# Expert gates brought to the features' partitions by DRAM transfers, and max-with-0 and gate product as one DVE operation

## Chip, cores and metric

The kernel runs on one core of a Trainium2 chip. The metric is the device time of one execution in microseconds (us). The core's engines work in parallel, each through its own queue in order: PE (matrix products), DVE (vector operations), ACT (functions and copies), POOL (a second, general vector engine) and SP, which here only issues DMA transfers. SBUF and PSUM are the on-chip memories; matrix products end in PSUM[...].

## What is computed

Eight layers run over an input of 8 blocks of 512 tokens with 128 features, in fp32. The change concerns the sixth, an expert layer with 32 experts of 64 features each, of which every token uses four. Cut to what matters:

```python
def _L2_ffn_ref(x, expert_sel, keys, values):   # x: tokens x 128
    sel_logits = jnp.einsum('nd,ed->ne', xt, expert_sel)
    gates = jax.nn.sigmoid(sel_logits)
    sel_val, sel_idx = jax.lax.top_k(gates, 4)
    gate_full = jnp.zeros_like(gates).at[jnp.arange(N)[:, None], sel_idx].set(sel_val)
    scores = jax.nn.relu(jnp.einsum('nd,edf->nef', xt, keys))
    scores = scores * gate_full[:, :, None]
    out = jnp.einsum('nef,efv->nv', scores, values)
    return out.reshape(B, S, -1)
```

and `x = x + _L2_ffn_ref(_layernorm(x), ...)`. All 32 experts are computed for all tokens; the 28 gates that weren't chosen are zero. The seventh layer, a scan over time, follows.

## The kernel before

The function l2_ffn_l3_attn (L1138) holds the sixth and the seventh layer. Its first part, from L1336, is the stage of this study. It works block by block (b from 0 to 7). Features stand on the partitions and the 512 tokens of a block along the free dimension. Two experts of 64 features fill the 128 partitions, so a block has 16 pairs (j from 0 to 15).

For each pair: PE multiplies the pair's keys with the normalised block xT (L1432) into a PSUM tile mm; ACT takes the maximum with 0 into act (L1436); DVE multiplies act with the gates (L1444); and PE adds the pair's value product to acc (L1421, in add_up). The list late holds pairs whose value product isn't issued yet: it is issued once more than one pair waits, so that PE computes key products ahead.

The gates must stand on the feature rows: each of the two experts' gates, one number for each token, on 64 partitions. For this PE multiplies a 0/1 matrix sel with the transposed gates gT (L1443), for four pairs at once (every fourth j), in four PSUM tiles sp. The four products use 32 rows of the array each, so that gT holds the gates four times, on rows 0, 32, 64 and 96. POOL builds sel once, ahead of the stage (L1341, L1344).

The gates come from route(b) (L1371), a generator: normalise, transpose, logits on PE, sigmoid on ACT, then four times first_max (L1350) on DVE, which finds and removes the largest gate of each token; then the gates are copied four times (full4, L1393), transposed on PE and copied by ACT into gT (L1399). route(0) runs ahead of the loop; route(b + 1) runs beside block b. Such generators lie in the list side, and each pair ends with step(side) (L1448), which lets each of them run to its next yield. Others there: give_back (L1404: acc is transposed, added to X, and the statistics for the next norm are taken on DVE), folded, and prepare (L1273), which makes the scan's inputs for blocks 0 and 1 beside blocks 5 and 6: a chain on PE, ACT and then POOL, which ends with two writes to DRAM on SP's queue, dt_d (4 MB, L1327) and du_d (2 MB, L1331).

The code states an order of issue; the compiler orders the instructions of each engine by it and by when it expects their inputs, and each engine then runs its queue in order. PSUM in this stage: two tiles mm (shared by key products and everything in side), two acc, four sp.

After the stage the scan begins (L1455), which reads dt_d and du_d back in transfers dr, gx and xk (fetch, L1466).

Of the kernel before, what the change touches and what calls it, by code (L numbers as in the profile page):

```python
# [15 lines left out]
F32 = mybir.dt.float32  # L16
AF = mybir.ActivationFunctionType
ALU = mybir.AluOpType
# [21 lines left out]
def eight_layers(ctx: ExitStack, tc: tile.TileContext, w: dict, out: bass.AP):  # L40
# [184 lines left out]
    def flipped(src, ps, dst, scale=None):  # L225

        for c in range(C):
            nc.tensor.transpose(ps[:, c, :], src[:, c, :], ident)
        flat = ps.rearrange("p c t -> p (c t)")
        if scale is None:  # L230
            nc.scalar.copy(dst, flat)
        else:
            nc.scalar.activation(dst, flat, AF.Copy, scale=scale)
# [904 lines left out]
    def l2_ffn_l3_attn():  # L1138
# [18 lines left out]
        with ExitStack() as es:  # L1157
# [178 lines left out]
            with ExitStack() as es2:  # L1336
                ffn = es2.enter_context(tc.tile_pool(name="f2", bufs=2))
                ps2 = es2.enter_context(tc.tile_pool(name="f2p", bufs=2, space=PSUM))

                sel = ffn.tile([P, 4, 2, 64], F32, tag="sel", name="sel", bufs=1)  # L1340
                nc.gpsimd.memset(sel, 1.0)  # L1341
                for k in range(4):
                    at = sel[32 * k : 32 * k + 32]
                    nc.gpsimd.affine_select(  # L1344
                        out=at, in_=at, compare_op=ALU.is_equal, fill=0.0, base=-2 * k,
                        pattern=[[-8, 4], [-1, 2], [0, 64]], channel_multiplier=1,
                    )
                ready = {}

                def first_max(sc, last):  # L1350
# [20 lines left out]
                def route(b):  # L1371
                    r = rstd_of(mv2, b)
                    yield True
                    xn = ffn.tile([P, C, D], F32, tag="xn", name="xn")
                    normal(b, mv2, r, xn)
                    yield True
                    xT = ffn.tile([P, S], F32, tag="xT", name="xT")
                    flipped(xn, mm_four(), xT)
                    yield True
                    lp = mm_four()[:, :, 0:E]  # L1380
                    for c in range(C):
                        nc.tensor.matmul(lp[:, c, :], xT[:, cols(c)], f2_sel, start=True, stop=True)
# [11 lines left out]
                    nc.vector.tensor_tensor(  # L1394
                        full4, full.unsqueeze(2).to_broadcast([P, C, 4, E]),
                        oh.unsqueeze(2).to_broadcast([P, C, 4, E]), ALU.add,
                    )
                    yield True
                    gT = ffn.tile([P, S], F32, tag="gT", name="gT")  # L1399
                    flipped(full4.rearrange("p c k e -> p c (k e)"), mm_four(), gT)  # L1400
                    ready[b] = xT, gT
                    yield True

                def give_back(b, acc):  # L1404
                    oT = ffn.tile([P, S], F32, tag="oT", name="oT")
# [7 lines left out]
                    yield True  # L1413

                finish(route(0))
                side = [folded()]
                late = []

# [4 lines left out]
                        side.append(give_back(b, acc))  # L1423

                for b in range(NB):
                    xT, gT = ready.pop(b)
                    if b < NB - 1:
                        side.append(route(b + 1))
                    acc = ps2.tile([P, S], F32, tag="acc", name="acc")
                    for j in range(J):  # L1430
                        mm = mm_tile()
                        nc.tensor.matmul(  # L1432
                            mm, f2_k[:, 2 * j : 2 * j + 2, :], xT, start=True, stop=True
                        )
                        act = ffn.tile([P, S], F32, tag="act", name="act", bufs=4)
                        nc.scalar.activation(act, mm, AF.Relu)  # L1436
                        if len(late) > 1:
                            add_up()
                        if j % 4 == 0:
                            sp = [ps2.tile([P, S], F32, tag="sp", name="sp", bufs=4) for k in range(4)]  # L1440
                            for k in range(4):
                                at = slice(32 * k, 32 * k + 32)
                                nc.tensor.matmul(sp[k], sel[at, j // 4], gT[at], start=True, stop=True)  # L1443
                        nc.vector.tensor_tensor(act, act, sp[j % 4], ALU.mult)  # L1444
# [281 lines left out]
```

## Time and profile before

| What | Value |
|---|---|
| Median of 3 runs | 2018.02 us (2016.74 to 2020.12) |
| Profiled execution | 2007.65 us |
| Its span, first to last instruction | 2005.9 us |
| Mean granted clock of PE | 0.853 |
| Busy shares: PE, DVE, ACT, POOL | 83%, 64%, 41%, 33% |
| Stage of this study: first key product to last value product | 953.6 to 1262.9 us of the span |

A line of the timeline has the start in us, the duration in us, the engine, the line of code, the operation, what it writes and reads, shapes and how often, and in brackets how long the engine was idle before it and what ended that. Product groups with x2 are one fp32 product in two passes. A line of groups ends with busy time and mean duration in ns, and the idle time just before the group with what released it. PE's products overlap, so that its busy time can't be added up; starts can.

### The profile page before, as it was taken

To read this page: it belongs to the slowest core of one execution; us is meant where nothing else is said; L and a number is where in the kernel's file an instruction comes from. 1 tells how busy PE (TensorE), PEld (TensorE's weight loads), DVE (VectorE), ACT (ScalarE), POOL (GpSimd) and SP (SyncE) were. 2 spreads that over 40 slices of the span, in tenths; PEclk is the share of its full clock that TensorE was granted. 3 is DMA by queue.
4 is the path that set the end of the run, shared out by engine and by line. 5 is a ranking of instruction groups with operands and counts; after the bars stand their busy time and mean duration, and the time that the engine had idled before them with its cause. 6 is when DMAs were issued, how large, how long until landed. Compare 5 with 4: busy or idle time off the path is not lost.

```text
span 2005.9 us, 24650 instructions
## 1 busy us (share of the span) xinstructions
PE 1661.1 (83%) x9157; PEld 688.7 (34%) x9157; DVE 1283.0 (64%) x2369; ACT 826.5 (41%) x1197; POOL 655.8 (33%) x708
## 2 busy tenths in 40 slices
PE   6978988999989775785999999698768788698774
PEld 2322333434444363554434444112112112122353
DVE  5656666566655422454565554498878779798489
ACT  4645555544534221442323343345445346345221
POOL 5544433432211204303020054516245244211152
PEclk8989989888999997776999999758778778677788
DMA  8970000000000272000000024653864855842000
GB/s 277 383 222 1 1 1 11 17 10 9 21 16 17 88 223 61 18 1 0 1 0 1 0 79 173 193 156 107 227 192 92 246 169 131 236 111 74 1 16 27
DMA packets 118345, 181.02 MB, mean 90 GB/s; under 512 B 11464, under 2 KB 43088, under 8 KB 118224
## 3 DMA queue, kind: packets, MB, share of 16 engines
q1 hardware_dynamic: 116176, 175.24, 29.4%
q0 software_dynamic: 2048, 4.20, 0.7%
q8 instruction: 72, 1.18, 0.2%
q14 instruction: 49, 0.40, 0.1%
HBM read 74.55 MB, written 96.47 MB: 85 GB/s over the span
## 4 chain that ended last, share of the span: by engine, by line
PE 24%; DVE 14%; issue 5%; DMA 4%; POOL 4%; ACT 1%; SPq 1%; DVEq 0%; POOLq 0%; ACTq 0%
DVE h L1599 5%; PE bx L1588 5%; PE mm L1432 4%; PE acc L1421 4%; DMA dr<-dt_d 3%; PE Z L1501 3%; PE sp L1443 1%; POOL h L1637 1%; DMA gx<-du_d 1%; PE o L1641 1%; DVE act L1444 1%; DVE t L1652 1%; PE mm L1520 1%; SPq L1472 1%; DVE n L1654 1%
## 5 line engine op out<-in xcount | busy, mean ns | idle before, releaser
L1599 DVE TENSOR_TENSOR_SCAN h<-a,bx 128x1024 f32<-128x1024 f32 x192 | 427.9, 2270 | 98.4 <-ACT a L1594 53.0
L1594 ACT ACTIVATE a<-dr,nA 128x1022 f32<-128x1022 f32 x192 | 216.6, 1144 | 308.4 <-DVE h L1599 191.7
L1588 PE MATMUL bx<-gx,wb 32*64 32x512 f32 x1536 | 233.8, 814 | 94.0 <-DVE h L1599 55.1
L1444 DVE TENSOR_TENSOR act<-act,sp 128x512 f32<-128x512 f32 x128 | 87.6, 686 | 128.7 <-ACT act L1436 84.1
L1488 POOL TENSOR_TENSOR gx<-gx,xk 128x1024 f32<-128x1024 f32 x32 | 75.3, 2353 | 253.5 <-DMA gx<-du_d 222.4
L1501 PE MATMUL Z<-h,wc 64*32 64x512 f32 x1536 | 147.5, 830 | 10.5 <-DVE zx L1509 10.3
L1436 ACT ACTIVATE act<-mm 128x512 f32<-128x512 f32 x128 | 76.2, 597 | 164.7 <-PE mm L1432 155.7
L1421 PE MATMUL acc<-act,L_ffn_values 128*128 128x512 f32 x256 | 132.9, 602 | 8.2 <-DVE act L1444 8.1
L1432 PE MATMUL mm<-xT,L_ffn_keys 128*128 128x512 f32 x256 | 135.3, 610 | 0.0
L1588 PEld LDWEIGHTS bx<-gx,wb 32*64 32x64 f32 x1536 | 42.2, 159 | 260.3 <-DVE h L1599 182.5
L470 DVE TENSOR_REDUCE mx<-sm 128x8 f32<-128x1024 f32 x64 | 76.2, 1212 | 46.8 <-POOL sm L466 46.8
L498 POOL TENSOR_SCALAR_AFFINE_SELECT eT<-eT 128x1024 f32<-128x1024 f32 x64 | 68.6, 1095 | 105.6 <-ACT eT L496 105.5
L466 POOL TENSOR_SCALAR_AFFINE_SELECT sm<-sm 128x1024 f32<-128x1024 f32 x64 | 69.3, 1096 | 56.7 <-ACT sm L465 56.3
L496 ACT ACTIVATE eT<-sT 128x1024 f32<-128x1024 f32 x64 | 62.0, 1020 | 57.9 <-PE sT L489 57.8
L465 ACT COPY sm<-sc 128x1024 f32<-128x1024 f32 x64 | 63.0, 1013 | 51.3 <-PE sc L459 31.6
L1178 POOL TENSOR_TENSOR rstd<-rstd,minus_half 128x4 f32<-128x4 f32 x16 | 16.5, 1036 | 192.0 <-DVE rstd L1177 191.9
L459 PE MATMUL sc<-kb,qT 32*128 32x512 f32 x256 | 58.4, 736 | 22.4 <-ACT eT L496 10.2
L321 DVE SCALAR_TENSOR_TENSOR xn<-x,mv,rstd 128x128 f32<-128x128 f32 x128 | 45.9, 409 | 44.5 <-POOL rstd L317 44.4
L1421 PEld LDWEIGHTS acc<-act,L_ffn_values 128*128 128x128 f32 x256 | 47.1, 192 | 65.2 <-issue 46.5
L489 PE MATMUL sT<-qT,kb 32*128 32x512 f32 x256 | 57.1, 692 | 14.2 <-ACT sm L465 8.3
L1432 PEld LDWEIGHTS mm<-xT,L_ffn_keys 128*128 128x128 f32 x256 | 46.2, 192 | 65.2 <-issue 52.1
L199 DVE BATCH_NORM_STATS2 bn<-x 128x6 f32<-128x128 f32 x256 | 64.2, 271 | 6.5 <-DMA x<-in_L_attn_hidden_states 5.4
(411 smaller groups left out, 3203.9 us busy)
## 6 DMA issues: line engine op xcount, KB each, us to landing
f_in<-we SPq DMA_DIRECT2D x10, 3584.0 KB, 27.2
dt_d<-dt SPq DMA_DIRECT2D x8, 4096.0 KB, 13.0
dr<-dt_d SPq DMA_DIRECT2D x64, 512.0 KB, 7.9
du_d<-du SPq DMA_DIRECT2D x8, 2048.0 KB, 14.0
gx<-du_d SPq DMA_DIRECT2D x32, 512.0 KB, 6.5
wt<-in_L_ffn_experts SPq DMA_DIRECT2D x48, 192.0 KB, 2.8
xk<-xh SPq DMA_DIRECT2D x128, 64.0 KB, 6.1
xg<-f_in SPq DMA_DIRECT2D x48, 64.0 KB, 2.6
```

What stands on the lines that cost most here:

```text
L466: nc.gpsimd.affine_select(out=sm, in_=sm, compare_op=ALU.is_ge, fill=-1e30, base=0, pattern=[[0, 8], [-1, P]], channel_multiplier=1,)
L470: nc.vector.tensor_reduce(mx[:, c, 2 * i : 2 * i + 2, 0:4], sm.rearrange("p (q r) k -> p q r k", q=2), AX.X, ALU.max, negate=True,)
L498: nc.gpsimd.affine_select(out=e4, in_=e4, compare_op=ALU.is_ge, fill=0.0, base=0, pattern=[[0, 8], [1, P]], channel_multiplier=-1,)
L1421: nc.tensor.matmul(acc, f2_v[:, j, :], act, start=(j == 0), stop=(j == J - 1))
L1432: nc.tensor.matmul(mm, f2_k[:, 2 * j : 2 * j + 2, :], xT, start=True, stop=True)
L1436: nc.scalar.activation(act, mm, AF.Relu)
L1444: nc.vector.tensor_tensor(act, act, sp[j % 4], ALU.mult)
L1488: nc.gpsimd.tensor_tensor(gx, gx, xk.unsqueeze(1).to_broadcast([P, 2, S]), ALU.mult)
L1501: nc.tensor.matmul(zs[q][32 * j : 32 * j + 32, i, :], wc[half, g, :], hs[j // 2][half, j % 2, :], start=(g == 0), stop=(g == G - 1),)
L1588: nc.tensor.matmul(bx[64 * i : 64 * i + 64, k, :], wb[at, g, :], gx[at, i, :], start=True, stop=True,)
L1594: nc.scalar.activation(a[:, :, 1:], dr[:, 2 * j : 2 * j + 2, 1:], AF.Exp, scale=nA[:, q, g : g + 1],)
L1599: nc.vector.tensor_tensor_scan(h.rearrange("p r t -> p (r t)"), a.rearrange("p r t -> p (r t)"), bx.rearrange("p r t -> p (r t)"), 0.0, AL ...
```

## The change

The gates are transposed once, on 32 rows, copied to gT and written to DRAM (gd, 64 KB for each block). For each group of four pairs fetch_gates reads them back into a tile gate, twice 64 partitions, each row repeated 64 times: two transfers of 512 KB on SP's queue. It is issued two groups ahead, and there are three such tiles. At pair 8 of each block this asks for the next block's gates, so that route is stepped on until they are issued. sel, its products and full4 go. The maximum with 0 and the gates' product become one DVE operation that reads the key product from PSUM; ACT has no part in it. Key products get four PSUM tiles of their own (key) in place of sp. The value product lags by three pairs in place of two, and act has five buffers in place of four.

```diff
-                sel = ffn.tile([P, 4, 2, 64], F32, tag="sel", name="sel", bufs=1)
-                nc.gpsimd.memset(sel, 1.0)
-                for k in range(4):
-                    at = sel[32 * k : 32 * k + 32]
-                    nc.gpsimd.affine_select(
-                        out=at, in_=at, compare_op=ALU.is_equal, fill=0.0, base=-2 * k,
-                        pattern=[[-8, 4], [-1, 2], [0, 64]], channel_multiplier=1,
-                    )
...
                     full = first_max(gt, False)
-                    for k in range(1, 3):
+                    for k in range(1, 4):
                         yield True
-                        oh = first_max(gt, False)
+                        oh = first_max(gt, k == 3)
                         nc.vector.tensor_tensor(full, full, oh, ALU.add)
                     yield True
-                    oh = first_max(gt, True)
-                    full4 = ffn.tile([P, C, 4, E], F32, tag="full4", name="full4")
-                    nc.vector.tensor_tensor(
-                        full4, full.unsqueeze(2).to_broadcast([P, C, 4, E]),
-                        oh.unsqueeze(2).to_broadcast([P, C, 4, E]), ALU.add,
-                    )
-                    yield True
-                    gT = ffn.tile([P, S], F32, tag="gT", name="gT")
-                    flipped(full4.rearrange("p c k e -> p c (k e)"), mm_four(), gT)
-                    ready[b] = xT, gT
-                    yield True
+                    mm = mm_four()
+                    for c in range(C):
+                        nc.tensor.transpose(mm[0:E, c, :], full[:, c, :], ident)
+                    gT = ffn.tile([E, S], F32, tag="gT", name="gT", bufs=1)
+                    nc.scalar.copy(gT, mm[0:E].rearrange("p c t -> p (c t)"))
+                    gd = dram.tile([E, S], F32, tag="gates", name="gates", bufs=3)
+                    nc.sync.dma_start(gd, gT)
+                    ready[b] = xT, gd
+                    yield True
+
+                spread = {}
+
+                def fetch_gates(b, m):
+
+                    gd = ready[b][1]
+                    t = ffn.tile([P, 4, S], F32, tag="gate", name="gate", bufs=3)
+                    for k in range(2):
+                        nc.sync.dma_start(
+                            t[64 * k : 64 * k + 64],
+                            gd[8 * m + k : 8 * m + 8 : 2, :].unsqueeze(0).to_broadcast([64, 4, S]),
+                        )
+                    spread[b, m] = t
...
                 finish(route(0))
+                fetch_gates(0, 0)
+                fetch_gates(0, 1)
...
                     for j in range(J):
-                        mm = mm_tile()
+                        if j % 4 == 0:
+                            m = 4 * b + j // 4 + 2
+                            if m < 4 * NB:
+                                while m // 4 not in ready:
+                                    step(side)
+                                fetch_gates(m // 4, m % 4)
+                            gate = spread.pop((b, j // 4))
+                        key = ps2.tile([P, S], F32, tag="key", name="key", bufs=4)
                         nc.tensor.matmul(
-                            mm, f2_k[:, 2 * j : 2 * j + 2, :], xT, start=True, stop=True
-                        )
-                        act = ffn.tile([P, S], F32, tag="act", name="act", bufs=4)
-                        nc.scalar.activation(act, mm, AF.Relu)
-                        if len(late) > 1:
+                            key, f2_k[:, 2 * j : 2 * j + 2, :], xT, start=True, stop=True
+                        )
+                        act = ffn.tile([P, S], F32, tag="act", name="act", bufs=5)
+                        nc.vector.scalar_tensor_tensor(
+                            act, key, 0.0, gate[:, j % 4, :], ALU.max, ALU.mult
+                        )
+                        if len(late) > 2:
                             add_up()
-                        if j % 4 == 0:
-                            sp = [ps2.tile([P, S], F32, tag="sp", name="sp", bufs=4) for k in range(4)]
-                            for k in range(4):
-                                at = slice(32 * k, 32 * k + 32)
-                                nc.tensor.matmul(sp[k], sel[at, j // 4], gT[at], start=True, stop=True)
-                        nc.vector.tensor_tensor(act, act, sp[j % 4], ALU.mult)
                         late.append((b, j, act, acc))
```

More of the change, by code (lines that the diff above doesn't have):

```diff
@@ L1425, in l2_ffn_l3_attn @@
                 for b in range(NB):
[L1426 removed]
+                    xT = ready[b][0]
                     if b < NB - 1:
                         side.append(route(b + 1))
[L1429 removed]
+                    acc = ps2.tile([P, S], F32, tag="acc", name="acc", bufs=2)
                     for j in range(J):
[L1431 removed]
+                        if j % 4 == 0:
[6 more added lines that the diff above has]
+                        key = ps2.tile([P, S], F32, tag="key", name="key", bufs=4)
                         nc.tensor.matmul(
[L1433 removed]
+                            key, f2_k[:, 2 * j : 2 * j + 2, :], xT, start=True, stop=True
                         )
[L1435 to L1444 removed]
+                        act = ffn.tile([P, S], F32, tag="act", name="act", bufs=5)
[3 more added lines that the diff above has]
+                        if len(late) > 2:
+                            add_up()
                         late.append((b, j, act, acc))
```

## The prediction

> **What bounds the kernel now.** I read the page's engine shares first, then the groups by line, then the order of time on PE inside the stage that the change touches (the second expert layer, 953.6 to 1262.9 us of the span), then the waits, and last the transfers. The stage's own row and the groups:
>
> ```profile
> 950.00:1263.00 313.00, 299.50 (x949) 127.97 (x949) 171.62 (x454) 102.92 (x176) 65.80 (x77) 0.98 0.11 41
> L1432 PE MATMUL mm<-xT,L_ffn_keys 128*128 128x512 f32 x256 | 135.3, 610 | 0.0
> L1443 PE MATMUL sp<-gT,sel 32*128 32x512 f32 x256 | 42.6, 644 | 0.0
> L1444 DVE TENSOR_TENSOR act<-act,sp 128x512 f32<-128x512 f32 x128 | 87.6, 686 | 128.7 <-ACT act L1436 84.1 <-PE sp L1443 44.6
> ```
>
> The columns of the first are PE, weight loads, DVE, ACT, POOL, then clock, DMA share and GB/s. PE is busy for 299.5 of 313 us at a clock of 0.98, DVE for 172, ACT for 103, and the transfers use 11%. DVE waits for PE and ACT, so PE sets the pace. Busy time overlaps, so I take PE's pace from the starts:
>
> ```profile
> 1062.48 1.14 PE L1443 MATMUL sp<-gT,sel 32*128 32x512 f32 x8
> 1063.55 1.13 PE L1432 MATMUL mm<-xT,L_ffn_keys 128*128 128x512 f32 x2
> 1064.51 1.02 PE L1421 MATMUL acc<-act,L_ffn_values 128*128 128x512 f32 x2
> 1065.37 1.02 PE L1432 MATMUL mm<-xT,L_ffn_keys 128*128 128x512 f32 x2
> ...
> 1068.80 1.02 PE L1432 MATMUL mm<-xT,L_ffn_keys 128*128 128x512 f32 x2
> 1069.66 1.02 PE L1421 MATMUL acc<-act,L_ffn_values 128*128 128x512 f32 x2
> 1070.61 1.14 PE L1443 MATMUL sp<-gT,sel 32*128 32x512 f32 x8
> ```
>
> A pair of experts (one key product, one value product) takes 1.715 us: 1065.37 to 1068.80 is two of them. A group of four pairs with its gate products takes 1070.61 - 1062.48 = 8.13 us, so these cost 8.13 - 4 x 1.715 = 1.27 us of PE's time, with nothing beside them. Where PE does stand still, DVE is behind:
>
> ```profile
> 1049.89 1.13 PE L1421 MATMUL acc<-act,L_ffn_values 128*128 128x512 f32 x2 [2.48 <-DVE act L1444]
> 1055.05 0.63 PE L228 MATMUL mm<-ident,full 128*128 128x128 f32 x4 [0.54 <-DVE full L1394]
> ```
>
> That is the burst of top-four selections (first_max) in pairs 4 to 8 of each block. The stage's account: 309.3 = 128 x 1.715 (219.5) + 32 x 1.27 (40.6) + the side products (routing 1.75 x 7, giving back 0.44 x 8, prepare 5.7 x 2, the folded weights 0.6: 27.8), which leaves about 21 us of waits, of which 18 are such bursts and the rest the cold start and the tail.
>
> **What the Trainium skill says.** "VectorE: DVE Perf Modes", section on why PSUM operands drop a tier: a PSUM operand holds an fp32 operation at one element per cycle. The trace agrees for the operation removed (686 ns for 512 with one operand in PSUM). "SBUF — State Buffer", section on who interferes with whom: a DVE operation with at most one SBUF input doesn't contend with GpSimd. Both the old and the new multiplication have one; no run here isolates it. "DMA: Bandwidth & Descriptors", section on queues, rings and completion order: a sequencer's transfers go into one ring per engine and are consumed in ring order. The trace agrees: du_d, 2 MB, issued 1.35 us after the 4 MB dt_d, lands after 14.0 us and dt_d after 13.0. "TensorE: Matmul & The Clock Gate", section on what is actually happening: after an idle window of about 3.4 us the clock halves. The first key products agree: two passes from 953.56 to 955.41, 1.85 us in place of 0.86.
>
> **The change part by part.**
>
> *Gate products go.* 32 groups x 1.27 us. The first lies in the start-up, which I treat apart: 31 x 1.27 = -39.4 us, all on PE's path.
>
> *ACT's maximum goes, DVE's operation changes.* DVE does 128 operations as before. The new form (three operands, key in PSUM) isn't there at 512; L1652, all in SBUF, takes 684 ns, L1117 with PSUM takes 342 at 128 where the same operation in SBUF takes 290 to 338. I take 0.69 us; the bounds are 0.68 and 0.74. DVE's sum stays near 170 us, below PE's. ACT loses 128 x 0.6 us, which lay beside PE: nothing by itself, but the way from key to act is some 0.8 us shorter. Key products get four PSUM tiles of their own (the four of sp), so that side products no longer share two with them; the 7.1 us that weight loads of L1432 waited for ACT's act are small pieces beside running products, and I count nothing for them. full4 (0.69) becomes an addition of 0.28.
>
> *Start-up.* Now:
>
> ```profile
> 934.57 2.89 POOL L1344 TENSOR_SCALAR_AFFINE_SELECT sel<-sel 32x512 f32<-32x512 f32 x4
> 937.54 3.12 POOL L1178 TENSOR_TENSOR rstd<-rstd,minus_half 128x4 f32<-128x4 f32 x3
> 953.81 0.58 ACT L231 COPY gT<-mm 128x512 f32<-128x512 f32 x1 [10.52 <-PE mm L228]
> 956.95 0.69 DVE L1444 TENSOR_TENSOR act<-act,sp 128x512 f32<-128x512 f32 x1 [4.41 <-PE sp L1443]
> ```
>
> Building sel holds the power operation that starts routing: without it 2.5 us sooner, and 0.4 for full4, so gT is there at 954.4 - 2.9 = 951.5. Then gates go to DRAM (64 KB; f_in->xg takes 2.6, xT 2.0: I take 2.3) and come back (two issues of 0.58, landing after some 7.5, from dr's rows below): about 961.4, and the first value product at 962.3. By then four key products are done, 4 of the block's 32. The old kernel had 4 of 32 done at 961.84. So +0.5, and +1.5 for a clock that may fall while PE waits: **+2**.
>
> *The steady supply.* A group's gates are 1 MB in two transfers, of the same size and packets as dr's:
>
> ```profile
> dr<-dt_d SPq DMA_DIRECT2D x64, 512.0 KB, 7.9
> 1266.00:1276.00 10.00, 6.25 (x28) 2.03 (x26) 0.19 (x2) 3.05 (x5) 4.43 (x5) 1.00 0.91 211
> dt_d<-dt SPq DMA_DIRECT2D x8, 4096.0 KB, 13.0
> du_d<-du SPq DMA_DIRECT2D x8, 2048.0 KB, 14.0
> ```
>
> In the second line, where such reads fill the engines to 0.91, they give 211 GB/s: 1.05 MB in 5.0 us, below the 6.9 us of a group. With three buffers, the transfer starts when DVE has finished the group two before and has 13.7 us less DVE's lag of 2 to 6. It fits with a landing of 8. The source is four rows read 64 times each; the nearest such read, out_proj_b (64 KB from one row of 512 B), lands in 2.9 us, and out_proj_w of the same size without repetition in 3.2. I take no penalty. The new waits: on SP the fetch waits for the gates' write and for a buffer, with only later fetches and prepare's writes queued behind it; on DVE act waits for its gate, and behind it stand the selections, the additions to X and, for PE, the value product three pairs later.
>
> *Bursts.* In pairs 4 to 8 DVE has about 2.3 us of selection to each 0.69 of product, against PE's 1.715. The gate products gave PE two pieces of other work there (2.5 us) and go; sums that lag by three pairs in place of two (1.7) and the shorter way (0.8) return as much. But the transposition of the gates now stands before pair 8's key product, because the fetch of the next block's gates must follow it. If PE really waits there, up to 2.8 us of cover (key, value and gate products at 1051 to 1054) are lost per block: at most +20 over seven blocks. If the deeper queues absorb the bursts, -10. I take **+6**.
>
> *Gates behind prepare's writes.* SP also issues dt_d and du_d, which wait for POOL. In the trace dt_d went out 7.0 us after block 6 began (1192.00 against 1185.02); with blocks shorter, about 9. A fetch behind both on SP is issued near 14 and drains behind 15.4 us of writes: landing at 28 to 29 us. In block 6 group 2 is wanted at about 23 and PE can run 3.5 on: 2 us lost. In block 7, without side work, it is wanted at 15.3 and PE runs 4 on: 9 lost. If SP issues the fetch first, nothing. Between 0 and +11; I take **+5**. Were a fetch of group 1 behind them, each would cost 16.
>
> After the stage nothing changes; the scan's loads wait for its last products as now.
>
> *Sum:* -39.4 + 2 + 6 + 5 = **-26.4 us**. The profiled execution has a span of 2005.9 and took 2007.65, 10 below the median of 2018.02. I subtract from the median: **1992**.
>
> **Rivals.**
> 1. Everything hides: bursts cost what they cost now, fetches go ahead of prepare's writes: -39.4 + 2 = -37, with absorption down to -47: **1981**. For it: 11% DMA share. Against: DVE's bursts already stop PE.
> 2. PE waits for DVE at the transposition and for gates in blocks 6 and 7: -39.4 + 2 + 20 + 11 = -6: **2012**. For it: the 2.48 us wait above.
> 3. Slower: gate supply becomes the bound. Repeated reads of the same 8 KB by 16 engines could be slower than 211 GB/s. An old group takes 309.3 / 32 = 9.67 us; the change loses once 1.05 MB takes longer than that, below 108 GB/s. At 100 GB/s, 32 x 10.5 = 336: +27, **2045**. For it: no read of this shape at this size in the trace. Against: out_proj_b.
>
> **How the numbers follow.** Forecast 0.50 (its own range 1980 to 2004), rival 1 0.15, rival 2 0.17, rival 3 0.18. Range 1970 to 2022: rival 1's absorption to rival 2 with a fetch one group later; most of rival 3 is left out. A measurement can tell 0.2% (4 us). Rivals 1 and 2 and the forecast are faster except a tail of rival 2: faster 0.77, same 0.05, slower 0.18.
>
> **What would show it.** No sp row; group periods near 6.9 us; DVE's act at 0.69; first act near 961; gate landings near 8 us; waits of PE for DVE in pairs 4 to 8 and at the transposition; act waiting for a gate in block 7 after dt_d. Wrong would be: landings of 10 us and more in every group with DVE waiting for DMA, or PE waits of over 7 us per block.

## The result and the profile after

The changed kernel takes 1996.7 us (median of 4 runs, 1995.6 to 1998.0), the kernel before on the same chip 2018.9 us (4 runs, 2016.7 to 2020.1): a ratio of 0.9891, 95% interval 0.9874 to 0.9909, or 22 us less. The forecast was 1992 us, the range 1970 to 2022.

The new rows of the stage, first of the groups by line, from the reference point to the end of the stage (busy us, mean ns, then idle time just before and what ended it):

```profile
L1443 PE MATMUL key<-xT,L_ffn_keys 128*128 128x512 f32 x256 | 135.6, 614 | 0.0
L1425 PE MATMUL acc<-act,L_ffn_values 128*128 128x512 f32 x256 | 134.8, 611 | 19.6 <-DVE act L1447 19.6
L1447 DVE SCALAR_TENSOR_TENSOR act<-key,gate 128x512 f32<-128x512 f32 x128 | 85.5, 685 | 98.2 <-PE key L1443 51.0 <-DMA gate<-gates 41.3 <-PE mm L228 5.7
```

and of the transfers (KB each, median us from issue to landing):

```profile
gate<-gates SPq DMA_DIRECT2D x64, 512.0 KB, 10.3
gates<-gT SPq DMA_DIRECT2D x8, 64.0 KB, 1.6
```

No sp row is left. DVE's fused operation takes 685 ns, as its predecessor did (686). New are 41.3 us in which DVE waits for gates (36.7 of them in blocks 6 and 7, 4.6 once in block 1), and 19.6 us in which a value product of PE waits for DVE: the forecast has to be checked there. In the middle of the stage PE runs as forecast; the order of time on PE:

```profile
1021.30 1.02 PE L1425 MATMUL acc<-act,L_ffn_values 128*128 128x512 f32 x2
1022.16 1.02 PE L1443 MATMUL key<-xT,L_ffn_keys 128*128 128x512 f32 x2
1023.02 1.02 PE L1425 MATMUL acc<-act,L_ffn_values 128*128 128x512 f32 x2
```

A pair takes 1.72 us (1021.30 to 1023.02) with nothing between pairs, so a group takes 6.9 us in place of 8.13. Block 3 as a whole, from its first value product to that of block 4, in the view by stretches, first before, then after (length, busy PE, weight loads, DVE, ACT, POOL, clock, DMA share, GB/s):

```profile
1074.40:1111.50 37.10, 35.71 (x118) 15.31 (x117) 22.20 (x64) 11.59 (x20) 2.90 (x5) 1.00 0.00 0
```

```profile
1065.60:1095.60 30.00, 30.00 (x88) 14.14 (x87) 20.63 (x66) 2.12 (x5) 2.79 (x5) 1.00 0.65 139
```

PE was busy for 35.71 of 37.10 us, and is now busy all the time for 30.00 us. The transfers fill 0.65 of the engines and hide.

To see where the rest went I took the start of each block's first value product, counted from one point that both kernels share: the first of the last four operations of L1117, in which the attention layer before the stage adds to X (932.57 us before, 937.53 after; the 5 us between them lie in code that is the same in both). After the stage both take the same again, 743.1 and 743.7 us. The time from this point to the last line of the table is called the length of the stage below.

| us from the reference point | before | after | difference |
|---|---|---|---|
| first value product of block 0 | 25.1 | 33.2 | |
| of block 1 | 64.1 | 63.5 | -0.6 |
| of block 6 | 258.0 | 222.2 | five blocks: -35.2 |
| start of the last value product's second pass | 329.7 | 312.1 | two blocks: +18.2 |
| sum | | | -17.6 |

The stage gains 17.6 us in the traces, and the medians differ by 22. The traces don't explain the other 4 us. They are no more than code that is the same varies by: the part after the stage takes 739.6 to 747.0 us in the traces of all kernels here.

Blocks 1 to 5 gain 7 us each on average (6.3 to 8.4), blocks 6 and 7 lose 18 us together though their eight groups of products are gone too. These two blocks by stretches:

```profile
1159.70:1178.00 18.30, 15.30 (x50) 7.60 (x49) 15.31 (x45) 2.93 (x4) 11.64 (x14) 0.96 0.65 240
1178.00:1191.00 13.00, 9.00 (x17) 3.54 (x14) 0.67 (x2) 4.34 (x6) 5.39 (x6) 0.76 1.03 266
1191.00:1208.50 17.50, 17.42 (x36) 7.50 (x36) 4.58 (x8) 0.59 (x1) 12.65 (x12) 0.83 0.42 126
1208.50:1224.10 15.60, 0.03 (x2) 0.02 (x1) 2.84 (x12) 0.00 (x0) 1.02 (x1) 0.57 0.97 273
1224.10:1250.20 26.10, 26.10 (x56) 11.24 (x56) 9.70 (x15) 0.00 (x0) 0.00 (x0) 0.93 0.68 179
```

PE does nothing for 15.6 us (1208.5 to 1224.1) and stands for 4 in the second stretch; after each stop its clock is down (0.76, 0.83, 0.93 as means), so that products of 0.86 us a piece take longer. The cause stands in the order of SP, which issues both the gates and prepare's writes:

```profile
1165.31 0.56 SPq L1327 DMA_DIRECT2D dt_d<-dt  x1
1166.67 3.15 SPq L1331 DMA_DIRECT2D du_d<-du  x1
1169.91 10.73 SPq L1400 DMA_DIRECT2D gate<-gates  x4
1180.74 1.40 SPq L1389 DMA_DIRECT2D gates<-gT  x1
1203.17 0.55 SPq L1327 DMA_DIRECT2D dt_d<-dt  x1
1203.82 8.68 SPq L1400 DMA_DIRECT2D gate<-gates  x4
1212.62 1.32 SPq L1331 DMA_DIRECT2D du_d<-du  x1
1214.05 14.19 SPq L1400 DMA_DIRECT2D gate<-gates  x4
```

and in SP's waits in that window (total, times, longest):

```profile
SPq L1327 <- POOL dt L1325: 38.6, 2, 21.0
```

The write of block 7's gates to DRAM is issued at 1180.74. Not one of their eight fetches goes out in the 21.0 us after it: SP is in order, the next thing on it is dt_d of block 1, and POOL has dt ready only at 1203.1. In the first 12 us of these 21.0 the gates weren't all in DRAM yet: their write stood last in the queue, behind the writes of block 0 and the fetches of block 6, and the last packet of these transfers ends at 1194.5. After that nothing moves (the last two columns are DMA share and GB/s):

```profile
1194.00:1195.00 1.00, 1.00 (x3) 0.48 (x2) 0.00 (x0) 0.00 (x0) 0.94 (x2) 0.50 0.14 25
1195.00:1203.00 8.00, 8.00 (x17) 3.33 (x16) 2.76 (x4) 0.00 (x0) 7.54 (x7) 0.87 0.00 0
```

Then the fetches stand behind the 4 MB of dt_d in the engines as well, and the first acts of block 7 wait until 1223.

This order on SP is the compiler's. Counted by the yields in the code, the program asks for block 7's first two groups (at pairs 8 and 12 of block 6) before it comes to dt_d of block 1 (at the end of pair 12).

### The profile page after: what moved, and what is told of

Its sections match the earlier page's. It is cut to its first block, busy times and chain, and to the rows that moved or that the text cites. A ratio compares the mean times of both kernels' runs of the same rounds, so it can differ in the third digit from the quotient of the medians.

```text
span 1993.9 us, 24047 instructions
## 1 busy us (share of the span) xinstructions
PE 1617.9 (81%) x8901; PEld 683.3 (34%) x8901; DVE 1278.6 (64%) x2369; ACT 749.7 (38%) x1069; POOL 652.3 (33%) x703
## 4 chain that ended last, share of the span: by engine, by line
PE 29%; DVE 16%; issue 8%; DMA 5%; POOL 3%; ACT 3%; SPq 2%; DVEq 0%; ACTq 0%; POOLq 0%
DVE h L1606 7%; PE bx L1595 4%; PE acc L1425 4%; PE key L1443 4%; DMA dr<-dt_d 3%; PE Z L1508 2%; PE mm L1009 1%; POOL h L1644 1%; PE mm L228 1%; PE o L1648 1%; DVE t L1659 1%; DVE zx L1516 1%; PE mm L1527 1%; PE gu L971 1%; SPq L1479 1%
## 5 line engine op out<-in xcount | busy, mean ns | idle before, releaser
L1595 PE MATMUL bx<-gx,wb 32*64 32x512 f32 x1536 | 229.5, 794 | 110.1 <-DVE h L1606 68.1
L1425 PE MATMUL acc<-act,L_ffn_values 128*128 128x512 f32 x256 | 134.8, 611 | 19.6 <-DVE act L1447 19.6
L1447 DVE SCALAR_TENSOR_TENSOR act<-key,gate 128x512 f32<-128x512 f32 x128 | 85.5, 685 | 98.2 <-PE key L1443 51.0
L1443 PE MATMUL key<-xT,L_ffn_keys 128*128 128x512 f32 x256 | 135.6, 614 | 0.0
L459 PE MATMUL sc<-kb,qT 32*128 32x512 f32 x256 | 57.6, 726 | 23.6 <-ACT eT L496 10.2
L1443 PEld LDWEIGHTS key<-xT,L_ffn_keys 128*128 128x128 f32 x256 | 49.6, 198 | 58.8 <-issue 58.8
L199 DVE BATCH_NORM_STATS2 bn<-x 128x6 f32<-128x128 f32 x256 | 64.1, 271 | 6.5 <-DMA x<-in_L_attn_hidden_states 5.4
L1644 POOL TENSOR_TENSOR h<-h 128x512 f32<-128x512 f32 x32 | 46.9, 1493 | 58.1 <-ACT h L1643 58.1
L994 POOL DMA_INDIRECT back<-f_out,back_at x32 | 31.2, 976 | 104.8 <-issue 104.5
## 6 DMA issues: line engine op xcount, KB each, us to landing
gate<-gates SPq DMA_DIRECT2D x64, 512.0 KB, 10.3
```

What stands on the lines that cost most here:

```text
L1425: nc.tensor.matmul(acc, f2_v[:, j, :], act, start=(j == 0), stop=(j == J - 1))
L1443: nc.tensor.matmul(key, f2_k[:, 2 * j : 2 * j + 2, :], xT, start=True, stop=True)
L1447: nc.vector.scalar_tensor_tensor(act, key, 0.0, gate[:, j % 4, :], ALU.max, ALU.mult)
L1595: nc.tensor.matmul(bx[64 * i : 64 * i + 64, k, :], wb[at, g, :], gx[at, i, :], start=True, stop=True,)
L1644: nc.gpsimd.tensor_tensor(h[:, k, :], h[:, k, :], h[:, k, :], ALU.mult)
```

## The experiments

The state of my theory then (A): the removed products give what was forecast; the blocks' bursts of selections stopped hurting; some 4 us were lost at the start; and 20 to 27 us are lost because gates queue behind prepare's writes on SP. Rivals: the DMA engines are simply full for that time (B), three buffers for gates are too few (C), and the gain comes from deeper queues or the fused operation more than from the removed products (D). In these runs the kernel before took 2008 to 2012 us (other chips), so expectations in us are to be read as ratios: divide by 2018.9.

### The four writes on another queue

```diff
-                nc.sync.dma_start(dt_d, dt.unsqueeze(1).to_broadcast([P, 16, S]))
+                (nc.gpsimd if b < 2 else nc.sync).dma_start(dt_d, dt.unsqueeze(1)...)
...
-                nc.sync.dma_start(du_d, du.unsqueeze(1).to_broadcast([P, HD, S]))
+                (nc.gpsimd if b < 2 else nc.sync).dma_start(du_d, du.unsqueeze(1)...)
```

> The changed kernel, with the writes of dt_d and du_d of blocks 0 and 1 (those that fall into expert blocks 6 and 7) on POOL's queue in place of SP's; SP then issues only gates until the scan. Theory A (the gates of blocks 6 and 7 come late because they stand behind 6 MB of writes in SP's own queue, about 20 us of PE's waits with their half-clock products): most of it goes, 1976 to 1984 us, 12 to 20 below the changed kernel's 1996.7; the 12 to 16 us waits of DVE's act for gates shrink to under 4. Theory B (the 16 DMA engines are simply full for that time, whatever the queue): within 5 us of 1996.7, and the waits stay at 10 us or more. A bound between: with two queues served in turn, a group of 1 MB would take some 10 us in place of 5 while the writes run, against one used each 6.9 us, and the two groups of lead cover about 14 us of it.

Measured: 1965.3 us, ratio 0.9778 (0.9745 to 0.9812), better than the edge of A (1976 us, 0.979). SP's order and SP's waits in blocks 6 and 7 of this kernel:

```profile
1177.29 0.31 SPq L1389 DMA_DIRECT2D gates<-gT  x1
1182.48 17.26 SPq L1400 DMA_DIRECT2D gate<-gates  x8
```

```profile
SPq L1400 <- DVE act L1447: 23.0, 5, 6.0
SPq L1389 <- ACT gT L1387: 18.4, 1, 18.4
```

The first fetch for block 7 goes out at 1182.5 and not at 1203.8, and what fetches wait for is now a buffer that DVE still reads, 6.0 us at most. DVE has no wait for gates in this window. Blocks 6 and 7 take 64.4 us in place of 89.9: **25.5 us** is what the shared order cost; the starts of all earlier blocks stay within 0.2 us. This takes away both parts of it at once, the wait for POOL at the head of the queue and the place behind the writes in the engines. A stands. B falls as the cause of the loss: the same bytes are written in the same two blocks. But by now all sixteen fetches of these two blocks go out before the write of dt_d next to them, so how fast gates would come through while 6 MB of writes run isn't shown. One small transfer was slowed: the write of block 7's gates, beside block 0's writes on the other queue, held the first fetch until 5.2 us after its issue (1177.29 to 1182.48), where for block 2's gates in the changed kernel this took 1.7 (1022.15 to 1023.82).

The same writes on ACT's queue (`nc.scalar` for `nc.gpsimd`):

> The changed kernel with the writes of dt_d and du_d of blocks 0 and 1 on ACT's queue in place of SP's. Theory A (what counts is that gates do not stand behind these writes in one queue): as with POOL's queue, which gave 0.978 of the kernel before, so 0.975 to 0.981; block 6 up to 3 us shorter than with POOL's queue if the 3.08 us operation of DVE beside POOL's issue there (0.29 us elsewhere) came from that issue. Rival (whoever issues into a full queue is held, on SP 3 to 6 us, and ACT's copies of xT, gT and oT stand behind it): 0.983 to 0.988, with PE waiting for xT or DVE for oT in blocks 6 and 7.

Measured: 1970.0 us, 0.9789 (0.9760 to 0.9818); blocks 6 and 7 take 66.1 us. Nearly the same gain, so it isn't a property of POOL's queue. Block 6 wasn't shorter (40.9 against 40.4 us): that guess was a miss.

The control, the same edit in the kernel before:

> The kernel before the change with only the writes of dt_d and du_d of blocks 0 and 1 moved to POOL's queue. A control: by theory A these writes cost nothing where no gates stand behind them, so 0.998 to 1.002 of the kernel before. If the move is worth something by itself (the scan's first loads, a shorter block 6 or 7): 0.985 to 0.995, and then the gain of that move on the changed kernel is not all the gates'.

Measured: 2012.0 us, 1.0003 (0.9990 to 1.0015), every block as in the kernel before within 0.1 us. The move is worth something only where gates stand behind these writes.

### More buffers, and fetches further ahead

```diff
-                    t = ffn.tile([P, 4, S], F32, tag="gate", name="gate", bufs=3)
+                    t = ffn.tile([P, 4, S], F32, tag="gate", name="gate", bufs=4)
```

> The changed kernel with four buffers for gates in place of three; every engine's order of instructions stays as it was. Theory C (three buffers hold the supply back: a fetch can be issued only when a group has been used): the waits of blocks 6 and 7 shrink by one group's 6.9 us each, 1982 to 1990 us. Theory A (the order on SP decides: block 7's fetches stand behind dt_d of block 1, which is ready only when POOL has made it): within 4 us of 1996.7, since SP reaches these fetches no earlier.

Measured: 1988.5 us, 0.9882 (0.9850 to 0.9913); blocks 6 and 7 take 88.7 us, 1.2 less than in the changed kernel, where C expected some 7 in each. C falls by the trace; by the time alone it would be open, since its range ends at 0.986.

With the same four buffers, fetches are given out three groups ahead:

```diff
+                fetched = 2
...
-                                fetch_gates(m // 4, m % 4)
+                            while fetched < min(m + 2, 4 * NB) and fetched // 4 in ready:
+                                fetch_gates(fetched // 4, fetched % 4)
+                                fetched += 1
```

> The changed kernel with four buffers for gates and fetches given out three groups ahead of use in place of two where the block's gates are ready. On SP's queue six of block 6's eight fetches then stand ahead of dt_d and du_d of block 0 (four before), and two of block 7's and du_d's order changes, while all of block 7's still stand behind dt_d of block 1. Theory A: block 6's wait (4.1 us and its slow products) goes and block 7's of 15.6 us stays: 1985 to 1993 us. Theory B: within 4 us of 1996.7. Theory C (buffers): 1980 to 1988.

Measured: 1989.1 us, 0.9896 (0.9865 to 0.9928): a miss of what I expected of A (0.983 to 0.987). Of PE's waits from 1155 us on, the main one:

```profile
PE acc L1426 <- DVE act L1450: 24.0, 2, 23.3
```

and SP's order:

```profile
1199.84 0.55 SPq L1327 DMA_DIRECT2D dt_d<-dt  x1
1200.48 10.96 SPq L1400 DMA_DIRECT2D gate<-gates  x6
```

Block 6's own wait for acts shrank as expected, to 0.7 us, but block 7's grew from 15.6 to 23.3 us. From the first value product of block 6 to that of block 7 it is 62.5 us in place of 64.4, which the fourth buffer alone had already given (62.4): the earlier fetches added nothing. PE came sooner to a point that didn't move: block 7's fetches still go out right behind dt_d, when POOL has made dt. I had taken the two waits as separate sums; they are one date.

### The fused operation, the depth, the products

The maximum back on ACT:

```diff
-                        nc.vector.scalar_tensor_tensor(
-                            act, key, 0.0, gate[:, j % 4, :], ALU.max, ALU.mult
-                        )
+                        nc.scalar.activation(act, key, AF.Relu)
+                        nc.vector.tensor_tensor(act, act, gate[:, j % 4, :], ALU.mult)
```

> The changed kernel with the maximum back on ACT (Relu from key to act, as before the change) and a plain product act*gate on DVE; gates still come by transfers. It separates the fused operation from the removed products. Theory A (the gain is that of the removed products, the fused operation is off the path): within 5 us of 1996.7, DVE's product 0.4 to 0.7 us, ACT busy up by about 80 us. Theory D (the shorter way from key to act makes the bursts harmless, and is worth some 10 us): 2003 to 2012 us, with PE's waits at the transpositions and behind act back to 4 us and more in each block.

Measured: 1989.4 us, 0.9900 (0.9868 to 0.9932); blocks 0 to 5 last 190.0 us (changed kernel: 189.0). The fused operation is worth nothing that can be measured here.

The deeper lag, alone, in the kernel before:

```diff
-                        act = ffn.tile([P, S], F32, tag="act", name="act", bufs=4)
+                        act = ffn.tile([P, S], F32, tag="act", name="act", bufs=5)
...
-                        if len(late) > 1:
+                        if len(late) > 2:
```

> The kernel before the change, with its value products held back by three steps in place of two and five buffers for act in place of four; gates still by products. It asks whether the changed kernel's shorter blocks (30.0 to 33.6 us from first value product to first value product in blocks 0 to 5, against 37.1 to 43 before, where the removed products alone account for 5.1 a block) come from the deeper lag. Theory D (the lag covers the bursts of DVE): PE's waits behind act shrink and blocks 0 to 5 get 1.5 us or more shorter each, 0.992 to 0.996 of the kernel before. Theory A (the bursts stop hurting because the product's own chain, key to Relu to spread gate to product, is gone): blocks within 0.5 us of before, 0.998 to 1.002.

Measured: 2012.5 us, 1.0018 (0.9999 to 1.0037). The blocks became longer, 239.4 us for blocks 0 to 5 against 232.9, with PE's mean clock at 0.92 to 0.96 in blocks 1 to 3. No part of the gain comes from the lag alone; why those blocks got longer I didn't settle.

The depth of the kernel before in the changed one (lag of two, act with four buffers, key with two PSUM tiles):

```diff
-                        key = ps2.tile([P, S], F32, tag="key", name="key", bufs=4)
+                        key = ps2.tile([P, S], F32, tag="key", name="key", bufs=2)
...
-                        act = ffn.tile([P, S], F32, tag="act", name="act", bufs=5)
+                        act = ffn.tile([P, S], F32, tag="act", name="act", bufs=4)
...
-                        if len(late) > 2:
+                        if len(late) > 1:
```

> The changed kernel with the depth of the kernel before: value products held back by two steps, four buffers for act, and two PSUM banks for key in place of four; gates by transfers and the fused operation stay. If depth absorbs the bursts of selections: PE waits behind act and at the transpositions again in each block, blocks 0 to 5 last 2 us or more longer each than in the changed kernel (189.0 us for six), 0.993 to 1.000 of the kernel before. If it is the shorter chain: within 0.5 us a block, 0.987 to 0.991.

Measured: 1997.0 us, 0.9934 (0.9916 to 0.9952), between the changed kernel and the kernel before. In the trace blocks 0 to 5 last 191.6 us in place of 189.0, 0.4 us a block and not the 2 I had expected of the depth, and the first value product comes 1.9 later. The depth, all three parts of it together, is worth some 5 us of the stage (317.2 against 312.1).

Then products of the size of the removed ones, with a result that nothing reads, were added to the changed kernel:

```diff
                             gate = spread.pop((b, j // 4))
+                            for k in range(4):
+                                at = slice(32 * k, 32 * k + 32)
+                                nc.tensor.matmul(mm_tile(), ident[at], xT[at], start=True, stop=True)
```

> The changed kernel with four products a group added whose result nothing reads: of the size of the removed ones (32 rows by 128 and 512 columns, xT by a slice of the identity), at the place in the loop where the removed ones stood, written to the shared PSUM tile; everything else stays, the gates still come by transfers. It prices the removed products by themselves, without ACT's maximum, lag or banks. The prediction's term is 1.27 us a group or 5.1 a block: theory A expects blocks 0 to 5 (189.0 us from first value product to that of block 6) to last 30 to 41 us longer, the waits of blocks 6 and 7 to take up some of theirs, 1.004 to 1.012 of the kernel before. Theory D (depth and the shorter chain are most of the gain and the products' time was largely cover for something else): under 20 us longer, 0.991 to 0.999.

Measured: 2057.3 us, 1.0235 (1.0200 to 1.0269); blocks 0 to 5 last 265.9 us, 76.9 longer and not 30 to 41. Neither theory had that. The order of time on PE in block 3 shows why, and after it the waits of PE's weight loads for PE itself in the stage:

```profile
1114.62 3.08 PE L1444 MATMUL mm<-xT,ident 32*128 32x512 f32 x8
1117.63 1.13 PE L1446 MATMUL key<-xT,L_ffn_keys 128*128 128x512 f32 x2
```

```profile
PEld mm L1444 <- PE mm L1444: 22.1, 29, 1.2
```

Four products take 1117.63 - 1114.62 = 3.01 us here; the kernel before did its four in 1063.55 - 1062.48 = 1.07. There they used four sets of 32 rows and four PSUM tiles, and the first passes of all four started within 0.02 us. Here they used the same four sets of rows but two tiles in turn, which side products also use: the second product waited for ACT to copy the gates out of its tile (until 1115.35), and the third and fourth for the first and second to end. So never more than two of the four overlapped, and this run doesn't price the removed products. Their price rests on the traces: 8.13 against 6.9 us a group, and 35.71 against 30.00 us of busy PE in block 3.

### The start

In the changed kernel the order of time at the start is this:

```profile
957.83 4.13 SPq L1400 DMA_DIRECT2D gate<-gates  x6
...
961.21 0.28 DVE L1343 TENSOR_REDUCE oh_m<-gt 128x4 f32<-128x128 f32 x1 [1.50 <-ACT gt L1375]
...
969.73 0.29 DVE L1381 TENSOR_TENSOR oh<-oh 128x128 f32<-128x128 f32 x1
969.94 1.88 DVE L1447 SCALAR_TENSOR_TENSOR act<-key,gate 128x512 f32<-128x512 f32 x3
...
970.76 1.14 PE L1425 MATMUL acc<-act,L_ffn_values 128*128 128x512 f32 x1
```

The first group's gates land at 965.3 (the trace's completion of its second transfer), but DVE is in the selections of block 1 from 961.21 to 970.02, one behind another, and the first act comes only then. To turn this round, block 1's scores were made to depend on the first acts:

```diff
                     nc.scalar.activation(gt, lp, AF.Sigmoid)
+                    if b == 1:
+                        nc.vector.scalar_tensor_tensor(
+                            gt[:, 0, 0:1], late[-1][2][:, 0:1], 0.0, gt[:, 0, 0:1],
+                            ALU.mult, ALU.add,
+                        )
```

> The changed kernel with block 1's selections tied to the first four acts by one small operation (0 x act added to one column of scores), so that DVE takes the first four acts before the sixteen selection steps of block 1 and not after. It asks how much of the late start is the transfer and how much DVE's order. By my reading the first gates have landed 965.3 - 937.5 = 27.8 us after the reference point and the first act starts only 32.4 after it: the first value product then moves from 33.2 to about 29 us and the stage gets 3 to 5 us shorter, 0.9865 to 0.9885 of the kernel before. Rival: block 1's gates are late in turn, or PE at half its clock gains nothing: 33 us moves but the start of block 1 (63.5) stays within 1 us, 0.988 to 0.991.

Measured: 1990.7 us, 0.9883 (0.9851 to 0.9916), which the interval can't tell from the changed kernel's 0.9891. The trace can. DVE and PE now:

```profile
971.68 1.89 DVE L1452 SCALAR_TENSOR_TENSOR act<-key,gate 128x512 f32<-128x512 f32 x3 [6.38 <-DMA gate<-gates]
```

```profile
972.42 2.07 PE L1430 MATMUL acc<-act,L_ffn_values 128*128 128x512 f32 x2 [5.96 <-DVE act L1452]
```

DVE waits for the transfer itself, which lands at 971.6. With the reference point at 943.06 the first value product comes after 29.4 us in place of 33.2, block 6 begins at 218.7 in place of 222.2, and the stage is 4.9 us shorter. So of the late start (33.2 against 25.1 us before) 3.8 us were DVE's order and the other 4.3 the way through DRAM.

Both mended, the four writes on POOL's queue and the acts first:

> The changed kernel with both: the four writes on POOL's queue and block 1's selections tied behind the first four acts. If the two losses are separate and add up (25.5 us of the stage by the queue, 4.9 by the order at the start): the stage, 312.1 us in the changed kernel, comes to 280 to 284, and the time to 0.974 to 0.978 of the kernel before. If the earlier start is lost again in block 6: stage 286, 0.977 to 0.980.

Measured: 1962.6 us, 0.9776 (0.9741 to 0.9812), with a stage of 282.8 us (by the queue alone 286.4). In the trace the two gains add up but for 1.3 us; in the time the second can't be told from nothing. With the gates' spreading kept, this and the two kernels with the queue alone are the fastest found, and the intervals don't part them.

### No supply at all

```diff
-                                fetch_gates(m // 4, m % 4)
-                            gate = spread.pop((b, j // 4))
+                            gate = ready[b][1]
...
-                            act, key, 0.0, gate[:, j % 4, :], ALU.max, ALU.mult
+                            act, key, 0.0, gate, ALU.max, ALU.mult
```

ready[b][1] is the transposed table as the kernel before made it. The kernel leaves out the spreading of each expert's gate to its rows.

> The changed kernel without the supply of gates: neither products nor transfers spread them, and the fused operation multiplies by the block's table of transposed gates as it stands (row p has the gate of expert p modulo 32, so the spreading of each expert's gate to its rows is left out). Lag, banks and selections are the changed kernel's. It shows where the expert stage would end if the supply cost nothing. Theory A: the two losses found (25.5 us in blocks 6 and 7, about 8 at the start, of which 4 are DVE's order) are nearly all that the transfers cost, so blocks 1 to 5 keep the changed kernel's length within 1 us each, and the stage of 312.1 us comes to 272 to 280, 0.970 to 0.976 of the kernel before. Rival (the transfers also slow the steady blocks, by DVE's or PE's waits for gates): blocks 1 to 5 each 1.5 us or more shorter, the stage under 268, below 0.969.

Measured: 1955.6 us, 0.9722 (0.9690 to 0.9753); the stage takes 280.0 us, at the edge of the 272 to 280 of A. Blocks 1 to 5 are not shorter than in the changed kernel but longer, 165.3 against 158.7 us together (A had said within 1 us each), so what the rival expected didn't come. Of PE's waits in the stage the main one is

```profile
PE mm L228 <- DVE full L1385: 14.2, 7, 4.8
```

PE at the transposition of the gates, where the table is made; 7.3 us of it lie in blocks 1 to 5. A kernel with waits of its own there can't clear the transfers by itself. The changed kernel's trace says more: in its blocks 1 to 5 DVE waits for gates once, 4.6 us, and no value product of PE waits for an act. Without any supply the first value product comes after 21.1 us, against 33.2 in the changed kernel: the whole start costs 12 us against this kernel, of which its slower blocks give back 7 by block 6. The stage of the kernel with both mended is within 2.8 us of this one's. In the time the two are further apart (0.9776 and 0.9722), with intervals that just overlap.

## Why the prediction was near, point by point

The time came within 5 us, but that was luck: two errors of opposite sign nearly cancelled, and the stage by itself gained 17.6 us where 26.4 were forecast. In the stage's account (16 experts' pairs and four groups a block, 5.08 us of products a block) the terms came out so:

| step of the prediction | forecast | the profiles |
|---|---|---|
| gate products | -39.4 | -39.4 (31 groups) |
| start-up, with the first group | +2 | +3.2 (block 0: -0.6 + 3.8) |
| bursts | +6 | -9.8 (blocks 1 to 5: -35.2 + 25.4) |
| gates behind prepare's writes | +5 | +28.4 (blocks 6 and 7: +18.2 + 10.2) |
| sum | -26.4 | -17.6 |

The last column's split takes 1.27 us a group as given, so its first row can't test that; the sum is measured.

*Gate products*: right, as far as the traces go (5.7 us less of busy PE in block 3, of which some is the modelled ends of products). The run made to confirm it priced something else.

*Start-up*: the transfer was right: gT forecast for 951.5 on the time axis of before, 951.2 measured (956.15 less 5.0); gates there by 961.4 forecast, 960.4 measured. Wrong was that the first act follows at once. I had put no other work of DVE there; the selections of block 1 stood ahead and cost 3.8 us.

*Steady supply*: right. Transfers of 512 KB at the start land every 2.47 us (967.81, 970.28, 972.75, 975.22), that is 212 GB/s against 211 forecast; the repeated rows cost nothing extra. The median of 10.3 us to landing is a queue of several transfers, not a slow one. Rival 3 had no ground.

*Bursts*: wrong in sign. PE's waits at the transposition in blocks 1 and 2 were 2.95 and 0.9 us, and none in blocks 3 and 4; the +6 came from charging up to 2.8 us a block there. In the traces PE stands idle in blocks 1 to 5 for 8.3 us before, mostly behind acts, and for 3.8 after. That is 4.5 of the 9.8; the other 5.3 are time in which PE was busy before, beyond 1.27 us a group. By the run with shallow queues, depth explains a smaller part (0.4 us a block), and neither the fused operation nor the lag alone explains any. The cause of the rest stays open. One candidate is that PE no longer waits with products for DVE to free their four tiles. Another is that key products no longer share two tiles with the side products: before, their weight loads waited 4.6 us in these blocks for ACT's act, and the forecast counted nothing for that. No run separates the two.

*Gates behind prepare's writes*: the mechanism was named and the size was more than five times the forecast. I had block 6 lose 2 us and block 7 nine, with the fetch of one late group behind both writes ("issued near 14"), and wrote of the case of an earlier group that "each would cost 16". The trace has that case: all eight transfers of block 7, its first group's too, stood behind dt_d of block 1. I took the earlier groups' fetches to be out by then, and this step failed: the program does ask for two of the four groups before dt_d, but in the compiler's order on SP all came after it, and an in-order queue waits until its head is ready. SP stood 21.0 us for POOL's dt before any of them. Even the gates' own write was held up in the same queue, and ended only near 1194.5. The own queue gives 25.5 us of the 28.4 back; the rest includes the 3.7 us for which PE still waits at block 6's transposition there.

The Trainium skill on ring order ("DMA: Bandwidth & Descriptors", section "Queues, rings and completion order"), which the prediction drew on, agreed again: the fetch issued at 1203.82, 0.65 us after dt_d, reached the first acts of block 7 only at 1223.3, 19.5 us later, where the first fetch at the start, with nothing ahead, took 7.5 (957.83 to 965.3). These 12 us come on top of the 21.0 for which SP stood.

## What to carry to other kernels

When a transfer is moved onto a queue that other stages also use, list what stands before it there at the moment it is wanted, and for each of these ask when its *data* is ready: an in-order queue is held by the slowest producer of anything ahead, even while the DMA engines are idle (8 us and more here). Look at the order in the trace, not in the program, since the compiler may have changed it. Test it by giving the other traffic its own queue; more buffers or earlier fetches in the same queue did next to nothing here (0.988 and 0.990, with 0.989 for the changed kernel and 0.978 for the own queue). And of a sum that comes out right, check each term against its own stretch of the trace before believing the model.

## What the runs showed of the hardware

Four products of 32 rows by 512 columns, on four different sets of rows and with a PSUM tile each, ran at the same time: 1.07 us for all four in the kernel before, where one product of 128 rows takes 0.86. With two tiles between them, so that each had to wait for its tile, they took 3.01.

With prepare's writes on POOL's queue, one small selection step of DVE (0.29 us elsewhere) took 3.08. From the order of time of that kernel:

```profile
1163.23 3.08 DVE L1354 TENSOR_TENSOR oh<-oh_eq,oh_f 128x128 f32<-128x128 f32 x1
1163.83 1.34 POOL L1329 TENSOR_TENSOR du<-dt,xt 128x512 f32<-128x512 f32 x1
...
1165.06 1.10 POOL L1287 TENSOR_TENSOR u<-x,rr 128x512 f32<-128x512 f32 x1
```

It ends at 1166.31, just after two operations of POOL that follow each other without a gap (1163.83 to 1166.16). It wasn't the issue of the DMA by itself, as I had guessed beforehand: that ended at 1163.86. The kernel with both mended shows the same (3.09 us at most for this line), the changed kernel and that with ACT's queue don't (0.29).

Other steps of the selection show the same on a smaller scale, without any write on POOL's queue. In the changed kernel six of the 176 steps with two operands in SBUF took 0.9 to 1.3 us; each ran beside an operation of POOL and ended 0.15 us after it. None of the other 170 took over 0.30, though 35 of them also lay beside operations of POOL. The fused operation, with one operand in PSUM, never took over 0.69, though 27 of its 128 lay beside POOL for more than 0.5 us. These figures agree with what the prediction says of DVE and POOL. That the two engines block each other when both operands of DVE lie in SBUF is still a reading of what coincides in time: no run isolates it, and it doesn't say which steps are hit.
